# A decoder layer on one core: output projections laid a batch later, W2 steps spread over nine batches, stores on two queues

## The chip, the cores and the metric

The kernel runs on one core of a Trainium2 chip, in float32 throughout. The metric is the device time of one execution in microseconds (us). A core has five engines that run side by side: PE (TensorE, matrix products), DVE (VectorE), ACT (ScalarE), POOL (GpSimd) and SP (SyncE, used here to start DMAs). PE writes to PSUM, a memory of eight banks; the other data lie in SBUF.

## The reference, cut to what matters

One pre-norm decoder layer over x of 16 batches by 112 tokens by 512 features, with 16 heads of 32. A self attention whose heads pass through a small matrix Wdown (32 by 32) and back through Wup, a cross attention over 375 context tokens a batch, and a gated feed-forward part with a Hadamard transform (fwht) between its two halves:

```
x = x + attn(_layernorm(x), Wq, Wk, Wv, Wo, Wdown, Wup)
x = x + xattn(_layernorm(x), ctx_2048, mask, ...)
x = x + ffn(_layernorm(x), W1, W2, W3)

# attn:   q_r, k_r, v_r = heads(x @ W.T) @ Wdown
#         y = softmax(q_r k_r / sqrt(32)) v_r @ Wup;  out = y @ Wo.T
# ffn:    hidden = silu(x @ W1.T) * (x @ W3.T)
#         out = fwht(hidden) @ W2.T
```

## The kernel before, in words

The 1,792 tokens are 14 tiles of 128. Four batches are a group (448 tokens). The residual x stays in `xr`, token by token; `xyT` holds the transposed features that the matrix products read.

*Folding.* Wdown and Wup are made into block-diagonal matrices `bd` (lines 698 to 711), transposed and multiplied (`block_products`, 822), and folded into the query, key and value weights (`fold`, 830). These are the first matrix products of the kernel, mixed with the transposes of the first normalised tiles. The normalised tiles come from `Norm.start` (792): statistics of each tile on DVE (L750, L751), a chain of twelve small DVE operations for the reciprocal root (`rstd_of`, 753), then one operation a tile (L776) into a `row` buffer, `xn`.

*The order of the work.* PE's order is that of the program text: `manual_schedule` is set for PE alone (1495). The instructions of the other engines are put in order by the framework's scheduler, by their place in the program and by when it expects their inputs and buffers. On each engine the order is then fixed. `Filler` (559) spreads other matrix work between the steps of an attention batch: `lay(b, us, *pieces, prepared=n)` (1522) queues pieces and runs batch `b`; `us` says how much of the queue goes between its steps.

*A batch of self attention* (`self_attention`, 986): scores on PE (L908); on DVE two reductions (L996) and two subtractions (L998); on ACT two exponentials (L1001); then, behind the second subtraction on DVE, the store of the batch before (a reciprocal L949 and a product L950) and `prepared` steps of W2. On PE: a first portion of filler, transposes of the exponentials (L1015), filler, transposes, filler, then the products with the values (L919) and the sums (L930).

*Fillers of the self attention.* Queries, keys and values of the next group (`features` L849, `token_rows` L881), transposes of the next normalised tiles (L810), W2's products with a Hadamard matrix (`w2_products`, L1433), and the output projection of finished tiles (`after_self`, 977). A projection needs a PSUM bank of tag `mm`, of which there are two; the bank comes free when DVE has added the result to `xr` (L981). After its last tile `after_self` starts the next norm.

*W2.* `w2_steps` (1444) is a generator of 36 steps. The first 24 each take a `row` buffer for a difference (L1463), make a sum in place (L1464), and let ACT copy the difference back (L1465). The last 12 combine the four parts of W2 (L1477 to L1488) and store blocks to DRAM. All 36 are spread by `prepared`; whatever is left is run out in the loop `for _ in w2_prep`. Once W2 is out, its buffers take the weights of the cross attention (`xk`, `xv`, `xq`, `xo`).

*Row buffers.* `row` (655) gives out four buffers of 128 by 512 under one tag. `xn` of every norm, `diff`, `a`, `e`, `g`, `beta`, `rep`, `d` and the output rows `o` share them.

*The end.* The feed-forward part runs in two passes over the tokens. `output_tile` (1619) transposes a tile of the result back, adds `xr` on DVE (L1625) and stores it by a DMA from SP (L1626), 14 times in all.

Of the kernel before, what the change touches and what calls it, by code (L numbers as in the profile page):

```python
# [14 lines left out]
AF = mybir.ActivationFunctionType  # L15
# [3 lines left out]
P = 128  # L19
# [11 lines left out]
GB = 4  # L31
# [553 lines left out]
def mixed(a, b, skip=0):  # L585

    a, b = iter(a), iter(b)
    for _ in range(skip):
        yield next(a)
    while True:  # L590
        took = [next(p, None) for p in (a, b)]
        if took[0] is None and took[1] is None:
            return
        yield sum(t for t in took if t is not None)
# [3 lines left out]
def finite_layer(  # L598
# [30 lines left out]
    nc = tc.nc  # L629
# [10 lines left out]
    def psum(tag, shape, bufs=2):  # L640
        return ps[""].tile(shape, F32, tag=tag, bufs=bufs, name=tag)

    def weight(name):
        return wt.tile([P, C, D], F32, tag="w", name=name)
# [10 lines left out]
    def row(name):  # L655
        return ln.tile([P, D], F32, tag="row", name=name, bufs=4)
# [5 lines left out]
    def load_weight(w, src):  # L662
        nc.sync.dma_start(out=w, in_=src.rearrange("(c p) n -> p c n", p=P))
# [14 lines left out]
    whole = [range((g * GT) // P, ((g + 1) * GT) // P) for g in range(NG)]  # L678
# [13 lines left out]
    ident = keep.tile([P, P], F32, name="ident")  # L692
# [4 lines left out]

    bd = [keep.tile([P, P], F32, name=f"bd{k}") for k in range(2)]
    bdm = [keep.tile([P, P], F32, name=f"bdm{k}") for k in range(2)]
    diag = ln.tile([P, (4 * TT * 2 + (B + B // 2) * C)], F32, tag="good", name="diag", bufs=1)  # L700
    diag = diag[:, :P].rearrange("p (i d) -> p i d", i=HG)
    nc.gpsimd.memset(diag, 0.0)
    for i in range(HG):
        nc.gpsimd.memset(diag[ts(i, DH), i, :], 1.0)
    for k in range(2):
        nc.vector.tensor_tensor(
            bd[k].rearrange("p (i d) -> p i d", i=HG),
            diag,
            small[:, k, :].unsqueeze(1).to_broadcast([P, HG, DH]),
            ALU.mult,  # L710
        )
# [36 lines left out]
    def stats(src, l, t):  # L748
        st = ln.tile([P, 6], F32, tag="st", name="st")
        nc.vector.bn_stats(st, src)  # L750
        nc.vector.bn_aggr(mv[:, l, t, :], st)  # L751
# [70 lines left out]
    def block_products(k):  # L822
        tr = psum("mm", [P, C, P])
        nc.tensor.transpose(tr[:, 0, :], bd[k], ident)
        nc.scalar.copy(bd[k], tr[:, 0, :])
        nc.tensor.matmul(tr[:, 1, :], bd[0], bd[k], start=True, stop=True)
        nc.scalar.copy(bdm[k], tr[:, 1, :])
        yield 0.5

    def fold(dst, src, block):  # L830

        for m in range(C):
            acc = psum("mm", [P, D])
            for j in range(C):
                if block is None:
                    nc.tensor.transpose(acc[:, ts(j, P)], src[:, j, ts(m, P)], ident)
                else:
                    nc.tensor.matmul(
                        acc[:, ts(j, P)], src[:, j, ts(m, P)], block, start=True, stop=True
                    )  # L840
            nc.scalar.copy(dst[:, m, :], acc)
            yield 0.9
# [46 lines left out]
    def project(w, t, into):  # L889
        acc = psum("mm", [P, D])  # L890
        for c in range(C):
            nc.tensor.matmul(  # L892
                acc, xyT[:, c, ts(t, P)], w[:, c, :], start=(c == 0), stop=(c == C - 1)
            )
            if c == 1:
                yield 1.75
        into(acc)
        yield 1.75
# [78 lines left out]
    def after_self(tiles, norm):  # L977

        for t in tiles:
            yield from project(  # L980
                wo, t, lambda acc: nc.vector.tensor_tensor(xr[:, t, :], acc, xr[:, t, :], ALU.add)  # L981
            )
            stats(xr[:, t, :], norm.l, t)
        norm.start(False)
# [73 lines left out]
    def output_bias():  # L1058


        rep = row("rep")
        repv = rep.rearrange("p (c m) -> p c m", c=C)
        for c in range(C):
            nc.gpsimd.tensor_scalar(repv[:, c, :], ones, bv[:, c : c + 1], None, op0=ALU.mult)
        yield 0.0
        acc = psum("mm", [P, D])
        for c in range(C):
            nc.tensor.matmul(
                acc, repv[:, c, :], xo[:, c, :], start=(c == 0), stop=(c == C - 1)
            )  # L1070
        nc.vector.tensor_tensor(rows["bo"], acc, rows["bo"], ALU.add)
        yield 3.5
# [328 lines left out]
    w2 = []  # L1401
# [15 lines left out]
    def w2_matrix():  # L1417
        h_a = ident
        n, k = 1, 0
        while n < P:  # L1420
            h_b = bd[k]
            a = h_a.rearrange("p (m two n) -> p m two n", two=2, n=n)
            o = h_b.rearrange("p (m two n) -> p m two n", two=2, n=n)
            nc.vector.tensor_tensor(o[:, :, 0, :], a[:, :, 0, :], a[:, :, 1, :], ALU.add)
            nc.vector.tensor_tensor(o[:, :, 1, :], a[:, :, 0, :], a[:, :, 1, :], ALU.subtract)
            h_a = h_b
            n, k = 2 * n, 1 - k
        return h_a

    def w2_products(h, w):  # L1430
        for c in range(0, UNITS, 2):
            acc = psum("mm", [P, D])
            nc.tensor.matmul(  # L1433
                acc, h, w[:, ds(c, 2)].rearrange("p c n -> p (c n)"), start=True, stop=True
            )
            nc.scalar.activation(
                w[:, ds(c, 2)].rearrange("p c n -> p (c n)"),
                acc,
                AF.Copy,
                scale=1.0 / math.sqrt(FF),  # L1440
            )
            yield 0.9
# [55 lines left out]
    n1 = [Norm(0, r) for r in read]  # L1498
    n2 = [Norm(1, r) for r in whole]
    n3 = [Norm(3, r) for r in whole]  # L1500
    grp = [Group(g) for g in range(NG)]
# [3 lines left out]
    for k in range(32):  # L1505
        nc.tensor.transpose(warm[:, 0, ts(k % HG, P)], ident, ident)

    n1[0].start(True)
    f.add(block_products(0), mixed(fold(wq, raws[0], bdm[0]), n1[0].transposes()))
    f.add(grp[0].queries(), fold(wk, raws[1], None))  # L1510
    f.drain()
# [5 lines left out]
    h = w2_matrix()  # L1517
    w2_prep = w2_steps()

    kv = []  # L1520

    def lay(b, us, *pieces, prepared=0):
        f.add(*pieces)
        self_attention(b, grp[b // GB], f, us, prepared)

    lay(0, 15.5, mixed(grp[1].queries(), w2_products(h, w2[0])))
    lay(1, 15.5, mixed(grp[1].keys(), w2_products(h, w2[1])), prepared=6)
    lay(2, 14, mixed(grp[1].values(range(3)), w2_products(h, w2[2])), prepared=6)
    n1[2].start(True)
    lay(  # L1530
        3,
        9.5,
        mixed(grp[1].values(range(3, GB)), w2_products(h, w2[3])),
        n1[2].transposes(),
        prepared=6,
    )

    lay(4, 10.5, after_self(whole[0], n2[0]), prepared=6)
    lay(5, 12, grp[2].queries(), prepared=3)
    lay(6, 13.5, mixed(grp[2].keys(), n2[0].transposes(), 4), prepared=3)  # L1540
    n1[3].start(True)
    lay(7, 15.5, mixed(grp[2].values(range(GB)), n1[3].transposes(), 4), prepared=3)

    lay(8, 14, after_self(whole[1], n2[1]), prepared=3)
    for _ in w2_prep:
        pass
    lay(9, 12, grp[3].queries())
    xk, xv, xq, xo = (weight(n) for n in ("xk", "xv", "xq", "xo"))
    load_weight(xk, c_wk_t)
    load_weight(xv, c_wv_t)  # L1550
    load_weight(xq, c_wq_t)
    load_weight(xo, c_wo_t)
    lay(10, 14, mixed(grp[3].keys(), n2[1].transposes(), 4))
    lay(11, 14, grp[3].values(range(GB)))

    kv.append(Keys(0))
    lay(12, 14, output_bias(), after_self(whole[2], n2[2]))
    lay(13, 11.5, mixed(kv[0].keys(), n2[2].transposes(), 4))
    lay(14, 10.5, kv[0].values())
    kv.append(Keys(1))  # L1560
    qs = [Queries(n) for n in range(B // 2)]
    lay(15, 6, qs[0].pieces())
    pending.store()
# [4 lines left out]
    prepared = []  # L1568
# [50 lines left out]
    def output_tile(p, k):  # L1619
        t = p.n * (2 * GT // P) + k  # L1620
        tr = psum("mm", [P, C, P])
        for c in range(C):
            nc.tensor.transpose(tr[:, c, :], p.out[c // 2][:, c % 2, ts(k, P)], ident)
        o = row("o")
        nc.vector.tensor_tensor(o, tr.rearrange("p c n -> p (c n)"), xr[:, t, :], ALU.add)  # L1625
        nc.sync.dma_start(out=out[ts(t, P), :], in_=o)  # L1626

    def run(*pieces):
        for p in pieces:
# [49 lines left out]
    for u in range(UNITS):  # L1679
        for i in range(2):  # L1680
            p.products(u, i)
            if 2 * u + i < per:
                output_tile(before, 2 * u + i)
# [6 lines left out]
    for k in range(GT // P, per):  # L1690
        output_tile(p, k)


@with_exitstack
def decoder_layer(ctx: ExitStack, tc: tile.TileContext, *args):
    nc = tc.nc
    flag = ctx.enter_context(tc.tile_pool(name="flag", bufs=1))
    unfit = flag.tile([1, 1], I32, name="unfit")
    finite_layer(tc, unfit, *args)
    with tc.If(nc.values_load(unfit, min_val=0, max_val=1, skip_runtime_bounds_check_because="a comparison gives 0 or 1") > 0):  # L1700
        general_layer(tc, *args)
# [49 lines left out]
```

## Time and profile before

| what | value |
|---|---|
| median of three runs | 1429.58 us (1428.09 to 1430.37) |
| profiled execution | 1425.9 us, its span 1423.7 us |
| granted TensorE clock, mean | 0.995 |
| PE busy, 0 to 22 us | 14.40 us |
| PE busy, 22 to 69.4 us | 45.96 of 47.4 us |
| PE busy, 69.4 to 346.9 us (self attention) | 264.4 of 277.5 us |
| PE busy, 346.9 to 1424 us | 1061.8 of 1077.1 us |

The profile is one execution of the program. Its lines name the engine, the source line (L12 is line 12 of the kernel) and the tiles written and read. PE counts two instructions for one float32 product and one for a transpose. "x16" after a line of the timeline means that sixteen instructions in a row are merged. What stands in brackets is the idle time before the first of them and the instruction that ended it. PE's granted clock is below 1 only in the first 22 us and in two later stretches, 143 to 164 us and 311 to 332 us.

### The profile page before, as it was taken

The numbers are of one execution on the slowest core, as the hardware profiler recorded it, in microseconds if no ns is written. First come the engines' busy times: TensorE is split into PE (matmuls) and PEld (weight loads), VectorE is DVE, ScalarE is ACT, GpSimd is POOL, SyncE is SP. The second block draws the span as 40 slices with busy tenths as digits, with TensorE's granted clock in tenths as the row PEclk, the third lists the DMA queues.
The fourth block names the chain that finished last, engine by engine and source line by source line (L and its number), as shares of the span: only waits on it lengthen the run. The fifth ranks groups of instructions, "written<-read, shape, count | busy, mean of one in ns | idle before, by whom it ended". The sixth has DMA issues, their size and how long they took to land.

```text
span 1423.7 us, 19012 instructions
## 1 busy us (share of the span) xinstructions
PE 1386.6 (97%) x8096; PEld 766.7 (54%) x8096; DVE 790.1 (55%) x1340; ACT 365.3 (26%) x560; POOL 30.0 (2%) x46
## 2 busy tenths in 40 slices
PE   7999898999999999999999999999999999999997
PEld 5554454546565656565556565454555555555554
DVE  4058977455665677667665557644734324434332
ACT  2255432324233323332333333111120001111000
POOL 2000010210001000000000000000000000000000
PEclk9999999999999999999999999999999999999999
DMA  8100026101104414321120011222113223521301
GB/s 297 59 1 30 1 75 229 60 23 44 37 30 145 153 37 166 129 97 52 52 82 22 23 35 56 89 89 89 59 63 115 88 96 111 186 102 59 119 1 53
DMA packets 49728, 115.89 MB, mean 81 GB/s; under 512 B 2896, under 2 KB 31584, under 8 KB 41188
## 3 DMA queue, kind: packets, MB, share of 16 engines
q1 hardware_dynamic: 48832, 112.96, 22.2%
q0 software_dynamic: 672, 1.62, 0.4%
q8 instruction: 65, 1.06, 0.3%
q14 instruction: 27, 0.22, 0.0%
q10 hardware_dynamic: 132, 0.02, 0.0%
HBM read 86.80 MB, written 27.79 MB: 80 GB/s over the span
## 4 chain that ended last, share of the span: by engine, by line
PE 90%; DVE 7%; ACT 1%; issue 1%; DMA 0%; DVEq 0%; ACTq 0%
PE mm L849 21%; PE mm L881 14%; PE gate L1349 12%; PE ys L1349 6%; PE mm L892 6%; PE gate L1285 6%; PE mm L1349 5%; PE sc L908 4%; PE ys L919 3%; PE ys L1285 3%; PE mm L1285 3%; PE sc L1015 2%; PE ys L930 2%; PE mm L810 1%; PE mm L1433 1%
## 5 line engine op out<-in xcount | busy, mean ns | idle before, releaser
L881 PE MATMUL mm<-xv,cT 128*125 128x512 f32 x384 | 173.3, 598 | 1.8 <-ACT v L886 1.8
L849 PE MATMUL mm<-cT,xk 128*128 128x375 f32 x512 | 168.8, 485 | 1.3 <-ACT kT L857 1.3
L849 PEld LDWEIGHTS mm<-cT,xk 128*128 128x128 f32 x512 | 95.5, 190 | 71.2 <-issue 11.6
L881 PEld LDWEIGHTS mm<-xv,cT 128*125 128x125 f32 x384 | 70.0, 187 | 81.3 <-issue 73.9
L1349 PE MATMUL gate<-t,f 128*128 128x448 f32 x256 | 101.4, 539 | 0.0
L1139 DVE TENSOR_SCALAR e<-sc,hi 125x896 f32<-125x896 f32 x64 | 70.8, 1144 | 48.6 <-PE sc L908 48.6
L949 DVE RECIPROCAL r<-ys 128x448 f32<-128x448 f32 x32 | 94.3, 2947 | 1.9 <-PE ys L930 1.9
L1142 ACT ACTIVATE e<-e 125x896 f32<-125x896 f32 x64 | 60.9, 951 | 115.5 <-DVE e L1139 82.7
L996 DVE TENSOR_REDUCE mx<-sc 112x8 f32<-112x896 f32 x32 | 33.4, 1084 | 96.7 <-PE sc L908 96.7
L1285 PE MATMUL gate<-h,f 128*128 128x448 f32 x224 | 86.6, 539 | 0.0
L1349 PE MATMUL gate<-xyT,f 128*128 128x448 f32 x192 | 80.1, 540 | 0.0
L1349 PE MATMUL ys<-t,f 128*128 128x448 f32 x192 | 77.4, 539 | 0.0
L1349 PEld LDWEIGHTS gate<-t,f 128*128 128x128 f32 x256 | 48.6, 190 | 47.6 <-issue 47.2
L865 DVE CUSTOM_DVE_ANT_0 junk<-kT 128x375 f32<-128x375 f32 x64 | 34.1, 533 | 64.2 <-ACT kT L857 64.2
L1162 DVE TENSOR_TENSOR es<-es,e 125x896 f32<-125x896 f32 x64 | 68.6, 1089 | 0.4
L1139 DVE TENSOR_SCALAR es<-sc,hi 125x896 f32<-125x896 f32 x32 | 36.6, 1147 | 52.6 <-PE sc L908 45.9
L1285 PEld LDWEIGHTS gate<-h,f 128*128 128x128 f32 x224 | 42.5, 190 | 41.3 <-issue 40.9
L886 ACT COPY v<-mm 125x512 f32<-125x512 f32 (+1 forms) x64 | 37.1, 580 | 104.9 <-PE mm L881 104.8
L908 PEld LDWEIGHTS sc<-q,kT 32*125 32x125 f32 x1536 | 46.2, 183 | 31.9 <-issue 20.5
L857 ACT ACTIVATE kT<-mm,bk 128x375 f32<-128x375 f32 x64 | 36.5, 572 | 91.9 <-PE mm L849 91.9
L892 PE MATMUL mm<-wo,xyT 128*128 128x512 f32 x112 | 52.1, 613 | 7.3 <-DVE xr L981 7.3
L881 PE MATMUL mm<-wv,xyT 128*112 128x512 f32 x128 | 58.0, 596 | 0.3 <-ACT v L886 0.3
(178 smaller groups left out, 1900.2 us busy)
## 6 DMA issues: line engine op xcount, KB each, us to landing
f<-blocks SPq DMA_DIRECT2D x46, 1024.0 KB, 4.8
blocks<-o SPq DMA_DIRECT2D x16, 1024.0 KB, 5.3
cT<-in_ctx SPq DMA_DIRECT2D x16, 750.0 KB, 4.9
o<-in_f_w SPq DMA_DIRECT2D x32, 256.0 KB, 3.2
w<-in_f_w SPq DMA_DIRECT2D x4, 1024.0 KB, 8.7
blocks<-w SPq DMA_DIRECT2D x4, 1024.0 KB, 4.7
out_y<-o SPq DMA_DIRECT2D x14, 256.0 KB, 4.7
xr<-in_x SPq DMA_DIRECT2D x2, 1024.0 KB, 10.2
```

The lines of the kernel that those rows point to most:

```text
L849: nc.tensor.matmul(acc[:, :n], w[:, c, ts(j, P)], src[:, c, :], start=(c == 0), stop=(c == C - 1))
L881: nc.tensor.matmul(acc[:n, :], src[:, c, :], w[:, c, :], start=(c == 0), stop=(c == C - 1))
L886: nc.scalar.copy(dst[:n].rearrange("p h r -> p (h r)"), acc[:n, :])
L892: nc.tensor.matmul(acc, xyT[:, c, ts(t, P)], w[:, c, :], start=(c == 0), stop=(c == C - 1))
L908: nc.tensor.matmul(views[i // 2][:, i % 2, j, :], k_of(i, j), q_of(i, j), start=True, stop=True)
L919: nc.tensor.matmul(y[ts(i, DH), j, :], v[:, HG * j + i, :], es[i // 2][:n, i % 2, j, :], start=first and j == 0, stop=last, skip_group_che ...
L949: nc.vector.reciprocal(r, sums)
L1139: self.clip = nc.vector.tensor_scalar(e[:KP], sc, -CLIP, hi[:, n : n + 1], op0=ALU.max, op1=ALU.min).ins
L1142: nc.scalar.activation(e[:KP], e[:KP], AF.Exp, scale=SCALE)
L1162: nc.vector.tensor_tensor(total, total, late[3][i][:KP], ALU.add)
L1285: nc.tensor.matmul(banks[m][bank], o[:, c, ts(m, P)], t[:, c, :], start=first and c == 0, stop=c == UNITS - 1, skip_group_check=True,)
L1349: nc.tensor.matmul(bank, o[:, s, k, :], t[:, k, :], start=first and k == 0, stop=k == 1, skip_group_check=True,)
```

## The change

It has seven parts.

1. An Exp on one column of `ident` goes to ACT ahead of everything else.
2. The statistics of the first norm are put behind the two products that make `bd` (`made`) on DVE.
3. The W2 steps: six in each of batches 1 to 4 and three in each of 5 to 8 become four in each of batches 1 to 9. The loop that runs out what is left, and with it the last stores of W2, moves behind batch 9.
4. `n1[2].start`, the norm of tiles 7 to 10, moves from behind batch 2 to before it. Its transposes stay in batch 3.
5. The output projections of tiles 0 to 2 move from batch 4 to 5, of tiles 3 to 6 from batch 8 to 9, of tiles 7 to 9 from batch 12 to 13. What they change places with: queries of group 2 (now batch 4), queries of group 3 (now batch 8), and the first cross keys with the output bias (now batch 12). The transposes of the norm after tiles 7 to 9 go into batch 14, with the first cross values.
6. The loads of the first two context blocks (`Keys(0)`, `Keys(1)`) are traced one batch earlier. The transposes of tiles 11 to 13 in batch 7 start after three pieces in place of four.
7. Output tiles of odd `k` are stored by a DMA from ACT in place of SP.

```
@@ -697,13 +697,15 @@
+    nc.scalar.activation(bdm[0][:, :1], ident[:, :1], AF.Exp)
     diag = ln.tile([P, (4 * TT * 2 + (B + B // 2) * C)], F32, tag="good", name="diag", bufs=1)
...
     for k in range(2):
-        nc.vector.tensor_tensor(
+        made = nc.vector.tensor_tensor(
             bd[k].rearrange("p (i d) -> p i d", i=HG),
@@ -1505,7 +1507,8 @@
-    n1[0].start(True)
+    with tc.issue_after(made.ins):
+        n1[0].start(True)
@@ -1524,40 +1527,40 @@
     lay(0, 15.5, mixed(grp[1].queries(), w2_products(h, w2[0])))
-    lay(1, 15.5, mixed(grp[1].keys(), w2_products(h, w2[1])), prepared=6)
-    lay(2, 14, mixed(grp[1].values(range(3)), w2_products(h, w2[2])), prepared=6)
+    lay(1, 15.5, mixed(grp[1].keys(), w2_products(h, w2[1])), prepared=4)
     n1[2].start(True)
+    lay(2, 14, mixed(grp[1].values(range(3)), w2_products(h, w2[2])), prepared=4)
     lay(
         3,
         9.5,
         mixed(grp[1].values(range(3, GB)), w2_products(h, w2[3])),
         n1[2].transposes(),
-        prepared=6,
+        prepared=4,
     )
-    lay(4, 10.5, after_self(whole[0], n2[0]), prepared=6)
-    lay(5, 12, grp[2].queries(), prepared=3)
-    lay(6, 13.5, mixed(grp[2].keys(), n2[0].transposes(), 4), prepared=3)
+    lay(4, 12, grp[2].queries(), prepared=4)
+    lay(5, 10.5, after_self(whole[0], n2[0]), prepared=4)
+    lay(6, 13.5, mixed(grp[2].keys(), n2[0].transposes(), 4), prepared=4)
     n1[3].start(True)
-    lay(7, 15.5, mixed(grp[2].values(range(GB)), n1[3].transposes(), 4), prepared=3)
-
-    lay(8, 14, after_self(whole[1], n2[1]), prepared=3)
+    lay(7, 15.5, mixed(grp[2].values(range(GB)), n1[3].transposes(), 3), prepared=4)
+
+    lay(8, 12, grp[3].queries(), prepared=4)
+    lay(9, 14, after_self(whole[1], n2[1]), prepared=4)
     for _ in w2_prep:
         pass
-    lay(9, 12, grp[3].queries())
...
     lay(10, 14, mixed(grp[3].keys(), n2[1].transposes(), 4))
+    kv.append(Keys(0))
     lay(11, 14, grp[3].values(range(GB)))
-    kv.append(Keys(0))
-    lay(12, 14, output_bias(), after_self(whole[2], n2[2]))
-    lay(13, 11.5, mixed(kv[0].keys(), n2[2].transposes(), 4))
-    lay(14, 10.5, kv[0].values())
+    lay(12, 12.5, mixed(kv[0].keys(), output_bias(), 4))
+    lay(13, 14, after_self(whole[2], n2[2]))
     kv.append(Keys(1))
+    lay(14, 12.5, mixed(kv[0].values(), n2[2].transposes(), 2))
@@ -1623,7 +1626,7 @@
-        nc.sync.dma_start(out=out[ts(t, P), :], in_=o)
+        (nc.scalar if k % 2 else nc.sync).dma_start(out=out[ts(t, P), :], in_=o)
```

## The prediction

> **What bounds the kernel now.** I read the page first, then the list of who waited for whom on PE, then a table by stage, then the order of PE and DVE inside the stages that lose time.
>
> The page: PE is busy 97% of the span.
>
> ```profile
> span 1423.7 us, 19012 instructions
> PE 1386.6 (97%) x8096; PEld 766.7 (54%) x8096; DVE 790.1 (55%) x1340; ACT 365.3 (26%) x560; POOL 30.0 (2%) x46
> ```
>
> So 37 us at most are idle on PE, and the change adds and removes no matmul: only holes can pay. PE's waits inside the self attention (60 to 345 us):
>
> ```profile
> PE mm L892 <- DVE xr L981: 7.3, 2, 4.0
> PE mm L810 <- ACT kT L857: 2.9, 1, 2.9
> PE sc L1015 <- ACT e L1001: 1.2, 1, 1.2
> PE mm L810 <- ACT xyT L811: 1.1, 1, 1.1
> ```
>
> The table by stage shows where they lie: batch 4 (from 143.20), batch 8 (217.30), batch 9 (239.00) and batch 13 (311.20); the columns after the name are busy time and count, then the granted PE clock. Two of the holes also pull the clock down.
>
> ```profile
> 143.20:163.70 20.50, 16.53 (x116) 8.32 (x112) 19.94 (x29) 8.43 (x12) 0.00 (x0) 0.92 0.00 1
> 217.30:239.00 21.70, 18.41 (x128) 9.31 (x124) 16.81 (x24) 3.71 (x4) 0.00 (x0) 1.00 0.55 204
> 239.00:256.80 17.80, 16.61 (x124) 9.14 (x120) 11.43 (x23) 5.63 (x8) 0.00 (x0) 1.00 0.56 214
> 311.20:331.80 20.60, 17.69 (x136) 11.46 (x132) 13.87 (x30) 7.65 (x11) 4.11 (x3) 0.92 0.00 0
> ```
>
> PE's timeline in batch 4 (start, length, what, idle before it): third tile of the output projection waits 3.97 us for a PSUM bank, and then runs at half clock, 3.59 us where 1.90 is usual.
>
> ```profile
> 151.13 0.93 PE L1015 MATMUL sc<-ident,e 112*112 112x112 f32 x8
> 156.03 3.59 PE L892 MATMUL mm<-wo,xyT 128*128 128x512 f32 x4 [3.97 <-DVE xr L981]
> 159.46 0.93 PE L1015 MATMUL sc<-ident,e 112*112 112x112 f32 x8
> 160.23 1.90 PE L892 MATMUL mm<-wo,xyT 128*128 128x512 f32 x4
> ```
>
> And DVE just before and in it. The reader is to see two things: six W2 steps (L1463, L1464) run only after PE's transposes released their rows at 138, although their batch began at 128; and the add that frees the bank (L981, 155.29) stands behind them.
>
> ```profile
> 125.36 0.54 DVE L776 TENSOR_SCALAR xn<-xr,seen,rstd 128x512 f32<-128x512 f32 x1
> 126.42 1.45 DVE L776 TENSOR_SCALAR xn<-xr,seen,rstd 128x512 f32<-128x512 f32 x3
> 138.20 0.69 DVE L1463 TENSOR_TENSOR diff<-w 128x512 f32<-128x512 f32 x1 [1.23 <-PE mm L810]
> 146.16 2.08 DVE L996 TENSOR_REDUCE mx<-sc 112x8 f32<-112x896 f32 x2
> 150.15 2.95 DVE L949 RECIPROCAL r<-ys 128x448 f32<-128x448 f32 x1
> 155.29 0.68 DVE L981 TENSOR_TENSOR xr<-mm,xr 128x512 f32<-128x512 f32 x1
> ```
>
> **The sum before.** Batch 2: 0.3. Batch 3: 0.3 + 1.1. Batch 4: 4.0, and 1.7 of slow clock (3.59 less 1.90). Batch 8: 3.3. Batch 9: 1.2. Batch 13: 2.9, and about 1.7 of slow clock (one group of four L849 took 2.53 where its neighbours take 1.43; two groups of transposes 0.7 more together). Sum 16.5 us. The opening loses more: queries start at 21.33.
>
> **What the Trainium skill says.** "TensorE: Matmul & The Clock Gate", Part 1: the clock falls to half after an idle window of some 3.4 us that runs freely, so the same hole may or may not cost it. The trace agrees in kind: a 2.91 us hole (batch 13) cost clock and a 3.29 us hole (batch 8) did not. "DMA: Bandwidth & Descriptors", Issuing engines are not separate DMA queues: DMAs of several engines run on the same 16 engines, and a second issuer only saves issue time. The issue here is 0.332 us for each store. "ScalarE: Activation LUTs", What ACT_TABLE_LOAD costs: a load belongs to a change of set. The trace has one load at 1.92 us (1.28 us long) and one at 886.96, none at the first Exp at 73.58.
>
> **Part by part.** *Exp at the head and the stores.* The Exp moves no load that is left, and ACT is idle until 11.11: nothing. The last four stores are issued 0.65 us apart from SP, which needs 0.332 each; the last is k=6, which stays on SP, and takes 4.7 us to land. Nothing; between -0.5 and +0.5 us. In the second pass ACT may wait for an odd row, but its copies have about 3 us of slack (three products of 1.08 before the bank is needed again): nothing.
>
> *Wdown blocks first.* Now PE waits 2.78 us for bd (L706, at 10.40, behind the statistics). Behind the landing of a_up (issue 1.28 + 6.7 = 7.98) bd could be there at 8.3. But the statistics then start at 8.35 in place of 6.37; their own work (2.95 + 2.15 + 0.48) puts the first xn at 13.9, where the first transpose is now too (13.94). Gain: the first fold is over by then, so the second starts at 14.45 in place of 14.82, and the chain of fold, copy and transpose behind it (1.84 us a round) brings the queries to 20.6: 0.7 us won. Bounds -0.3 (if a_up lands a microsecond later) and +1.0.
>
> *n1[2] a batch earlier, W2 steps at four.* Rows of tag "row" (four) are handed out in program order: xn of n1[2] was ready at 31 us, but came at 125, behind batch 2's sixth diff. Its new place is before batch 2. So it takes all four rows after batch 1 and keeps them till its transposes at the end of batch 3 (137.6). Batch 2's four steps and batch 3's four wait for that: eight from 138.2 in place of six. At the measured 8.0/6 = 1.33 us a step they end at 148.8, and batch 4's first reduction waits behind them, 4.7 us after its scores (144.15). In batch 9 a delay of 3.37 us (243.32 less 239.95) cost 1.20, since four pieces of queries (6.28 us) lie in front; batch 4 has just these now. So it loses 4.7 - 2.2 = 2.5, and 0.5 for a chance of slow clock. Bounds: 0 if the reductions are let in between the steps, 9 if the steps go one row at a time.
>
> *Projections of tiles 0 to 2 in batch 5.* DVE has no backlog there (batch 4: 4.1 softmax + 3.5 store + 4 x 1.22 = 12.5 us in a batch of over 16). L981 comes 9.8 us after the first reduction, as measured (146.16 to 155.97): two thirds of it are reductions, subtractions and the reciprocal. PE asks for the bank 7.9 us after the scores. 2.0 lost, 0.3 for clock. In batch 6 the keys put 7.6 us in front, enough for the norm's chain.
>
> *Tiles 3 to 6 in batch 9.* Before, in batch 8, five W2 operations stood ahead of L981 and cost 3.3. Now the last four steps hold eight; the last one waits for a row, so seven go ahead: 3.3 + 2 x 0.6 = 4.4, and 1.1 for clock. Bounds 0 and 6. Batch 10's keys hide the delay that cost batch 9 its 1.2.
>
> *Tiles 7 to 9 in batch 13, cross keys in 12.* No norm runs ahead of batch 12, so the 2.9 and 1.7 go. In 13 no W2 step is left: L981 ends 7.7 to 8.3 us after the reductions start, PE asks at 7.9: 0.3. In 14 the chain of rstd and xn (5.6 us behind the last tile, 3.4 of it under transposes, values and scores) delays the reductions by 2.2; three pieces (5.7 us) stand in front of exponentials that need 2.2 + 4.1: 0.6.
>
> *Loads.* xk to xo come after batch 9 or earlier, by 258 us at the latest, and land in about 12: 30 us before batch 12. cT of batch 0 still waits for batch 11's scores. SP has under 1 us of issues in any batch there. Nothing.
>
> **The sum after.** 0.3 + 1.4 + 3.0 + 2.3 + 5.5 + 0.3 + 0.6 = 13.4. Won 16.5 - 13.4 = 3.1 in the self attention and 0.7 at the head: 3.8. The profiled execution took 1425.9 (span 1423.7 and 2.2 around it) and would take 1422.1; the median of the runs is 3.7 higher, so 1425.8.
>
> **The rivals.** *B, the bank comes free in time.* If L981 is put directly behind the store (7.7 us), batches 5 and 9 lose nothing, and batch 4 loses 1.0 with the reductions let in: 0.3 + 1.4 + 1.0 + 0.3 + 0.6 = 3.6, won 12.9 + 0.7, 1416.0. For it: in batch 4 L981 was let in after three operations. Against: batch 8, after five.
> *C, given back.* The clock falls in all three holes (1.7 each: 3.2 more than taken) and the head wins nothing: 1429.7. For it: two of four holes cost clock before.
> *D, slower.* The eight held steps get their rows one by one: diff, add and ACT's copy (0.62) in a line, some 2.2 us with the waits. The reduction of batch 4 then starts at 155.8, 11.6 after its scores; 9.4 lost and 1.7 of clock in place of 3.0: 1433.9. It decides from about 2.0 us a step. Against: the six of batch 3 took 1.33.
> That the blocks are not earlier, since a_up's DMA is what they wait for, is inside the bound of the head.
>
> **How the numbers follow.** Main case 0.48 (own range 1423 to 1428), B 0.20, C 0.20, D 0.12. Faster by over 0.2% (2.9 us, about what a measurement of this kernel can tell from no change): 0.41 of the main case and B, 0.61. Within: 0.07 and 0.18, 0.25. Slower: D and the rest of C, 0.14. The range 1416 to 1431 leaves out D and about a third of B.
>
> **What would show it.** Held diffs (L1463) with no W2 step in batch 2; the first reduction of batch 4 some 4 us behind its scores; PE's waits for L981 of 2 us in batch 5 and 4 in batch 9; none in batch 12; bd before the first statistics and the queries at 20.6. If W2 steps do run in batch 2, rows are not handed out in order, and batch 4's loss is not there. If L981 stands elsewhere, B or C holds.

## The result and the profile after

The changed kernel takes 1433.07 us (median; 1431.62 to 1434.67), the kernel before on the same chip 1428.43 (1423.96 to 1431.22). The ratio is 1.0034, 95% interval 1.0023 to 1.0046: slower by a third of a per cent. The profiled execution has a span of 1430.7 us, 7.0 more than before, with nearly the same mean granted clock (0.994, before 0.995). The medians differ by 4.6 only, since the profiled execution of the kernel before (1425.9) was one of its faster ones; what follows explains the 7.0 between the two profiles. From here on the line numbers are those of the changed kernel unless the kernel before is named. They are two higher than before at the places that matter: the projection's product is L894 (was L892), its add L983 (L981), the copy of the self attention's keys L857 (L855; the L857 of the kernel before, in the prediction's list, is the copy of the cross keys).

The page after: the work is the same, PE has 2.8 us more busy time, and the rest of the 7 us is idle.

```profile
span 1430.7 us, 19016 instructions
PE 1389.4 (97%) x8096; PEld 767.2 (54%) x8096; DVE 789.2 (55%) x1340; ACT 365.4 (26%) x561; POOL 30.4 (2%) x46
```

PE's waits inside the self attention, after (60 to 345 us; who waits, for whom, then total, number and longest in us):

```profile
PE mm L894 <- DVE xr L983: 9.6, 2, 5.1
PE mm L812 <- ACT kT L857: 1.8, 2, 1.1
PE mm L812 <- ACT v L888: 1.2, 1, 1.2
PE mm L812 <- ACT xyT L813: 1.2, 1, 1.2
PE mm L851 <- ACT kT L857: 0.8, 1, 0.8
PE ys L921 <- ACT eT L1019: 0.7, 1, 0.7
PE sc L1017 <- ACT e L1003: 0.5, 1, 0.5
```

Two more lines of 0.3 each, for `v`, stand in the views of both kernels. Before, the first line was 7.3. The wait for the projection's add did not go: it moved with the projection and grew. Four lines with `kT`, `v` and `eT`, 4.5 us together, are waits for ACT's copies.

The batches show where the 7 us came from. The durations in this table are worked out from the starts of the scores (L908, now L910) in PE's timeline, in us; "start" is the first score of batch 0. The three columns at the right belong to experiments below.

| | before | after | e2 | e10 | e5 |
|---|---|---|---|---|---|
| start | 69.4 | 70.3 | 69.8 | 69.3 | 67.1 |
| batch 4 | 20.5 | 17.1 | 17.1 | 16.5 | 16.4 |
| batch 5 | 16.4 | 21.1 | 14.7 | 20.4 | 14.7 |
| batch 6 | 17.8 | 20.0 | 24.6 | 19.7 | 18.7 |
| batch 8 | 21.7 | 16.4 | 16.4 | 16.4 | 16.4 |
| batch 9 | 17.8 | 25.6 | 18.1 | 18.1 | 18.1 |
| batch 10 | 18.2 | 19.5 | 20.0 | 19.5 | 18.3 |
| batch 13 | 20.6 | 15.9 | 15.9 | 15.9 | 15.9 |
| batch 14 | 14.7 | 17.9 | 17.9 | 17.9 | 17.1 |

The batches left out (0 to 3, 7, 11, 12) differ by 0.1 us at most among these five. Summed from unrounded starts: head +0.9; batches 4 and 5, which changed places, +1.3; 6 +2.3; 8 and 9 +2.5; 10 +1.3; 12 to 14 -1.5; the end +0.2. That is the 7.0.

PE's timeline of the changed kernel in batch 5 and the hole of batch 9 (start, length, what; in brackets the idle time before it):

```profile
162.22 7.13 PE L894 MATMUL mm<-wo,xyT 128*128 128x512 f32 x16
169.20 0.93 PE L1017 MATMUL sc<-ident,e 112*112 112x112 f32 x8
174.62 3.64 PE L894 MATMUL mm<-wo,xyT 128*128 128x512 f32 x4 [4.49 <-DVE xr L983]
...
252.19 5.82 PE L894 MATMUL mm<-wo,xyT 128*128 128x512 f32 x8 [5.09 <-DVE xr L983]
```

It is the picture of batch 4 before. In batch 5 two tiles run, the third waits, and then the clock is at half: 3.64 for four instructions where 1.90 is usual, 5.82 for eight where 3.70 is. What DVE did in that time in batch 5:

```profile
162.33 2.09 DVE L998 TENSOR_REDUCE mx<-sc 112x8 f32<-112x896 f32 x2 [0.33 <-PE sc L910]
...
166.33 2.95 DVE L951 RECIPROCAL r<-ys 128x448 f32<-128x448 f32 x1
169.19 0.63 DVE L1465 TENSOR_TENSOR diff<-w 128x512 f32<-128x512 f32 x1
169.74 0.61 DVE L952 SCALAR_TENSOR_TENSOR xyT<-ys,r 128x448 f32<-128x448 f32 x1
170.27 0.68 DVE L1466 TENSOR_TENSOR w<-w 128x512 f32<-128x512 f32 x1
170.86 1.29 DVE L1465 TENSOR_TENSOR diff<-w 128x512 f32<-128x512 f32 x2
172.07 1.29 DVE L1466 TENSOR_TENSOR w<-w 128x512 f32<-128x512 f32 x2
173.27 0.69 DVE L1465 TENSOR_TENSOR diff<-w 128x512 f32<-128x512 f32 x1
173.87 0.69 DVE L983 TENSOR_TENSOR xr<-mm,xr 128x512 f32<-128x512 f32 x1
```

Seven operations of W2 (count the x after L1465 and L1466: 1, 1, 2, 2, 1) stand ahead of the add that PE waits for. In batch 9 there are eight, between 246.16 and 251.44. The first product had ended at about 166, so the add could have run at 169.2, behind the reciprocal. DVE was never idle here; its order was wrong for PE.

### The profile page after: what moved, and what is told of

Read it like the earlier page. It is cut to its first block, busy times and chain, and to the rows that moved or that the text cites. A ratio compares the mean times of both kernels' runs of the same rounds, so it can differ in the third digit from the quotient of the medians.

```text
span 1430.7 us, 19016 instructions
## 1 busy us (share of the span) xinstructions
PE 1389.4 (97%) x8096; PEld 767.2 (54%) x8096; DVE 789.2 (55%) x1340; ACT 365.4 (26%) x561; POOL 30.4 (2%) x46
## 4 chain that ended last, share of the span: by engine, by line
PE 88%; DVE 8%; ACT 2%; issue 1%; DMA 0%; ACTq 0%; DVEq 0%; POOLq 0%
PE mm L851 20%; PE mm L883 13%; PE gate L1351 12%; PE ys L1351 6%; PE mm L894 6%; PE gate L1287 6%; PE mm L1351 5%; PE sc L910 4%; PE ys L921 3%; PE ys L1287 3%; PE mm L1287 3%; PE ys L932 1%; PE sc L1017 1%; DVE st L752 1%; PE mm L1435 1%
## 5 line engine op out<-in xcount | busy, mean ns | idle before, releaser
L894 PE MATMUL mm<-wo,xyT 128*128 128x512 f32 x112 | 54.2, 635 | 9.6 <-DVE xr L983 9.6
L910 PEld LDWEIGHTS sc<-q,kT 32*125 32x125 f32 x1536 | 46.2, 183 | 31.9 <-issue 19.8
## 6 DMA issues: line engine op xcount, KB each, us to landing
xr<-in_x SPq DMA_DIRECT2D x2, 1024.0 KB, 10.5
```

What stands on the lines that cost most here:

```text
L894: nc.tensor.matmul(acc, xyT[:, c, ts(t, P)], w[:, c, :], start=(c == 0), stop=(c == C - 1))
L910: nc.tensor.matmul(views[i // 2][:, i % 2, j, :], k_of(i, j), q_of(i, j), start=True, stop=True)
```

## The experiments

A ratio is against the kernel before on the same chip. Where only a span is given, there is one run, and its parts are compared inside the trace.

**e1: the statistics first again.** The changed kernel, without the wait for `made`:

```
-    with tc.issue_after(made.ins):
-        n1[0].start(True)
+    n1[0].start(True)
```

> The changed kernel with the first statistics no longer put behind the Wdown and Wup blocks. Theory (the statistics, 2 us late, cost more than the earlier blocks bring): the first xn is there at 12.5 us in place of 14.5, PE's wait of 3.3 us for it goes, and the scores of batch 0 start at 69.4 in place of 70.3; span 1429.8. Rival (the head is neutral, the 0.9 us come from somewhere else): batch 0 still starts at 70.3.

Measured: span 1431.3. Batch 0 begins at 69.07, 1.2 us earlier, so the order at the head does cost (the last section compares all the heads). But batches 5 and 9 took 22.2 and 26.2 for 21.1 and 25.6, with the very same waits (4.49 and 5.09). In batch 5 the granted clock was 0.85 in place of 0.92. In batch 9 it was 0.87 in both, but more of the slow stretch fell on products (6.40 us for the eight behind the hole, 5.82 before this edit). The gain at the head is shown, and the total doesn't show it.

**e3: the norm of tiles 7 to 10 behind batch 2 again.** Only `n1[2].start(True)` moves back behind `lay(2, ...)`. It asks whether the held rows, which push W2 steps together, are what puts them ahead of the add.

> The changed kernel with the norm of tiles 7 to 10 started behind batch 2 again, as before. Theory (its four rows hold up the W2 steps of batches 2 and 3, which then run into batches 4 and 5): W2 steps run in batch 2 again, batch 4 loses its wait of 0.5 us, and the add of batch 5 comes after four W2 operations in place of seven, so its wait is 2.5 to 3 us in place of 4.5; span about 1428. Rival (the held rows cost nothing): batch 5 waits 4.5 us again; span 1430.5.

Measured: span 1431.2. Batch 4 takes 16.4 and loses nothing, so its 0.7 did come from the held rows. The wait of batch 5 did not move; PE's timeline of this kernel:

```profile
173.49 3.78 PE L894 MATMUL mm<-wo,xyT 128*128 128x512 f32 x4 [4.49 <-DVE xr L983]
```

Seven operations still stand ahead. My explanation for batch 5 fell: the steps' own place ahead of the projection decides, not their backlog.

**e2: the W2 steps behind the filler.** In `self_attention`, the steps are traced after the first portion of filler, so that the scheduler sees the projection's adds first:

```
             pending.store()
-            for _ in range(prepared):
-                next(w2_prep, None)
         first = max(0.45 * us, min(us, 5.5))
         f.fill(first)
+        with tc.issue_after(behind.ins):
+            for _ in range(prepared):
+                next(w2_prep, None)
```

> The changed kernel with the W2 steps of a batch traced behind the first portion of filler, so that on DVE they stand behind the adds that free the projection's PSUM banks. Theory (W2 operations ahead of the add are what PE waits for): PE's waits for the add in batches 5 and 9 (4.5 and 5.1 us) fall under 0.6 each, their slow clock (1.7 and 2.1) goes, batch 5 takes 15.5 us in place of 21.1 and batch 9 about 19 in place of 25.6; span about 1418.5. Rival (reductions, subtractions and the reciprocal alone make the add late): 2.5 us or more of wait is left in each; span about 1425.

Measured: 1424.09 against 1427.32, ratio 0.9977 (0.997 to 0.9984), now faster than before. DVE of this kernel in batch 5:

```profile
161.82 2.09 DVE L998 TENSOR_REDUCE mx<-sc 112x8 f32<-112x896 f32 x2 [0.34 <-PE sc L910]
...
165.82 2.95 DVE L951 RECIPROCAL r<-ys 128x448 f32<-128x448 f32 x1
168.69 0.63 DVE L983 TENSOR_TENSOR xr<-mm,xr 128x512 f32<-128x512 f32 x1
```

The add is done 7.5 us after the first reduction began (161.82 to 169.32), where the changed kernel took 12.2 (162.33 to 174.56). Batch 5 takes 14.7 and batch 9 18.1 (the table): both waits are gone. But 4.6 of it came back in batch 6, most of it as one wait:

```profile
189.30 1.08 PE L812 MATMUL mm<-ident,xn 128*128 128x128 f32 x4 [4.46 <-DVE xn L778]
```

The steps now run among the statistics of the norm that follows the projection, and `xn` comes at 188.61. A stall was removed and the next thing in DVE's queue became late.

**e4: no W2 steps in the projection batches.** Six each in batches 1, 2, 6 and 8, none in 5 and 9, with the loop that runs out the rest before batch 9. If the steps themselves are to blame, both batches must be as short as in e2.

> The changed kernel with the W2 steps of batches 5 and 9 given to batches 1, 2, 6 and 8 (six in each), so that the batches with projections have none. Theory (W2 operations ahead of the add): as in the run with the steps behind the filler, waits under 0.6 us in batches 5 and 9; ten held steps now end in batch 4, which waits 1 to 3 us for its exponentials; span about 1420. Rival (softmax and store alone make the add late): 2.5 us or more left in each; span about 1427.

Measured: span 1426.8. Batches 5 and 9 take 14.7 and 18.1, as in e2. But six steps in batch 2 wait for the rows that `n1[2]` holds, and more of them fall on batch 4, which takes 23.2 with a wait of 3.6 for its exponentials (expected 1 to 3) and a granted clock of 0.85, and batch 7 takes 23.4 with a wait of 2.1 for `v`. The cause in 5 and 9 is shown twice now; where the steps are put in their place matters as much.

**e7: the norm behind the projection later.** In the changed kernel, `after_self` no longer starts the norm. The next batch starts it under the same `issue_after` as the store, behind its own subtractions, and the transposes of batches 6, 10 and 14 come two pieces of filler later (the norm in the cross attention keeps its place):

```
+        late_norms.append(norm)
+
+    def started(norm):
+        late_norms.remove(norm)
         norm.start(False)
+        yield 0.0
...
         with tc.issue_after(behind.ins):
+            while late_norms:
+                late_norms.pop().start(False)
             pending.store()
...
-    lay(6, 13.5, mixed(grp[2].keys(), n2[0].transposes(), 4), prepared=4)
+    lay(6, 13.5, mixed(grp[2].keys(), n2[0].transposes(), 6), prepared=4)
```

> The changed kernel with the norms after a projection started behind the next batch's subtractions, and their transposes two pieces later; W2 steps as in the changed kernel. Theory (the norm's chain delays the exponentials, and ACT's copies that free PE's banks stand behind these): the waits of batches 6 (0.8 and 0.7), 10 (1.1) and 14 (1.2) for kT and v go, batch 6 takes about 18 us in place of 20.0 and batch 10 about 18.2 in place of 19.5; the waits for the add in 5 and 9 stay at 4.5 and 5.1; span about 1426. Rival (the banks are late for another reason): 1 us or more is still lost in each of the three; span about 1430.

Measured: span 1428.4. Batches 6, 10 and 14 take 18.7, 18.3 and 17.1 for 20.0, 19.5 and 17.9; the waits for `kT` and `v` are gone, a wait of 0.8 for `xn` is left. So the norm's chain did delay the exponentials. The edit moves the transposes too, but ACT shows that the exponentials and copies came earlier: in batch 6 the copy behind the second exponential ended 7.8 us after the first score (190.14 less 182.31), and 10.5 us after it in the changed kernel (192.81 less 182.34). How the norm delays them is seen in the changed kernel's batch 6. On DVE the chain's last operation stands between the two subtractions:

```profile
187.89 1.09 DVE L1000 TENSOR_TENSOR e<-sc,mx 112x896 f32<-112x896 f32 x1
188.89 1.45 DVE L778 TENSOR_SCALAR xn<-xr,seen,rstd 128x512 f32<-128x512 f32 x3
190.26 1.08 DVE L1000 TENSOR_TENSOR e<-sc,mx 112x896 f32<-112x896 f32 x1
```

On ACT the copy that frees the keys' bank stands behind the exponential of the second:

```profile
191.44 0.95 ACT L1003 ACTIVATE e<-e 112x896 f32<-112x896 f32 x1 [1.06 <-DVE e L1000]
192.29 0.52 ACT L857 COPY kT<-mm 128x448 f32<-128x448 f32 x1
```

And PE waits for the copy:

```profile
192.86 0.66 PE L812 MATMUL mm<-ident,xn 128*128 128x128 f32 x4 [0.66 <-ACT kT L857]
```

**e8: one block ahead of the statistics, all stores from SP.** PE's first need is Wdown's block alone, and `a_up` lands after `a_down`:

```
-    for k in range(2):
-        made = nc.vector.tensor_tensor(
+    def make_block(k):
+        return nc.vector.tensor_tensor(
...
+    made = make_block(0)
...
         n1[0].start(True)
+    make_block(1)
```

> The changed kernel with only the Wdown block ahead of the first statistics, the Wup block behind them, and all stores on SP again. Theory (it is Wup's block, whose load lands at 8.4 us, that holds up the statistics): the first xn is there at 12.8 us in place of 14.5, the scores of batch 0 start at 68.5 in place of 70.3. The stores: from DVE's last operation to the end of the span 6.8 us as with two queues, plus or minus 0.3. Rival (the landing of Wdown's block holds them up too, or two queues do shorten the end): batch 0 at 69.5 or later; the end over 7.3 us.

Measured: span 1429.9. Batch 0 begins at 68.69, 1.6 us earlier. The changed kernel's DVE at the head:

```profile
8.44 0.29 DVE L708 TENSOR_TENSOR bd<-diag,small 128x128 f32<-128x128 f32 x1 [1.61 <-DMA small<-in_a_up]
8.65 1.28 DVE L752 BATCH_NORM_STATS2 st<-xr 128x6 f32<-128x512 f32 x2
...
13.96 1.92 DVE L778 TENSOR_SCALAR xn<-xr,seen,rstd 128x512 f32<-128x512 f32 x4
```

and PE's:

```profile
10.18 1.13 PE L840 MATMUL mm<-bdm,raw_q 128*128 128x128 f32 x8 [0.48 <-DMA raw_q<-in_a_wq]
14.56 1.11 PE L812 MATMUL mm<-ident,xn 128*128 128x128 f32 x4 [3.26 <-DVE xn L778]
15.47 1.91 PE L840 MATMUL mm<-bdm,raw_q 128*128 128x128 f32 x8
```

The second block waits 1.61 us for `a_up`, and everything behind it with it. With one block ahead the first `xn` begins at 12.44, and PE's wait is 1.95.

**e6: the kernel before, with its W2 steps behind the filler.** The edit of e2 alone. It asks whether the order of the batches was needed at all.

> The kernel before, with the W2 steps traced behind the first portion of filler, nothing else. Theory (W2 operations ahead of the add, in the old order as in the new): the waits for the add in batches 4 and 8 (4.0 and 3.3 us) fall under 0.6, the slow clock of batch 4 (1.7) goes, batch 13 keeps its 2.9; span about 1415. Rival (the steps pushed back delay the softmax of batches 5 and 9): half of it is given back there; span about 1420.

Measured: 1419.97 against 1427.71, ratio 0.9944 (0.9928 to 0.9961). Batch 8 takes 18.1 for 21.7. Batch 4 gains only 1.7 us, for another wait stood behind the first:

```profile
154.31 3.10 PE L892 MATMUL mm<-wo,xyT 128*128 128x512 f32 x4 [2.17 <-DVE xyT L950]
```

Tile 2 of the projection contains tokens of batch 3, whose store is made in batch 4 itself. A projection in batch 4 thus depends on that store, and one a batch later doesn't. PE asks 8.9 us after the batch's first score (152.14 less 143.25), and the store ended 11.0 after it. But the store was that late because four W2 operations, held from batch 3, ran from 143.79 to 146.24, ahead of the first reduction. In batch 5 of e2, where the first reduction follows the scores directly, the store ends 9.1 us after the first score. So most of this wait is W2's as well, and what the order is worth once W2 is out of the way of the reductions too was not measured. Batches 4 and 5 together take 37.0 before, 36.7 here, 38.2 after the change, 31.8 in e2. The wait of 2.9 in batch 13, which the changed order removes, is still there (20.6 us, 15.9 after the change).

**e10 and e11: the two halves of the change apart.** e10 is the kernel before with the changed order of batches (parts 5 and 6 of the change, and the Exp of part 1, with 6 and 3 W2 steps, the statistics first, the norm in its old place and all stores from SP). e11 is the kernel before with four W2 steps in each of batches 1 to 9 alone.

```
-    lay(4, 10.5, after_self(whole[0], n2[0]), prepared=6)
-    lay(5, 12, grp[2].queries(), prepared=3)
+    lay(4, 12, grp[2].queries(), prepared=6)
+    lay(5, 10.5, after_self(whole[0], n2[0]), prepared=3)
...
-    lay(8, 14, after_self(whole[1], n2[1]), prepared=3)
+    lay(8, 12, grp[3].queries(), prepared=3)
...
+    lay(9, 14, after_self(whole[1], n2[1]))
```

> The changed kernel with only its order of batches left: head, W2 steps (six in batches 1 to 4, three in 5 to 8), norm of tiles 7 to 10 and stores as before. Theory (the order pays, and W2 steps in the batches with projections spoil it): batch 9, now with no step, takes 18.1 us in place of 25.6; batch 5 waits about 3.3 us behind five W2 operations and takes about 18.5; batches 6 and 10 keep their 20.0 and 19.5; span about 1419. Rival (the order itself is what loses): batches 4 to 14 together take as long as in the changed kernel, 209 us from the scores of batch 4 to those of 15; span about 1429.

> The kernel before with only the W2 steps spread as in the change, four in each of batches 1 to 9. Theory (what counts is how many operations stand ahead of the add): batch 4, with a smaller backlog and two operations ahead of the add in place of three, waits about 1.5 us in place of 4.0 and takes about 17 in place of 20.5; batch 8, with six ahead in place of five, waits about 4 in place of 3.3; span about 1420. Rival (spreading the steps is what loses in the change): batches 4 to 9 take longer than before (113.6 us from the scores of batch 4 to those of 10); span over 1424.

Measured for e10: 1422.27 against 1428.37, ratio 0.9957 (0.9943 to 0.9971). The order alone pays. It pays in batches 8 and 9, together 34.6 us for 39.5, because the projection of batch 9 now has no W2 step beside it, and in batches 12 to 14 (1.5). Batches 4 and 5 take 36.9 as before, and 6 and 10 lose 3.2. Batch 5, with three W2 steps, keeps a wait:

```profile
PE mm L894 <- DVE xr L983: 3.8, 1, 3.8
```

Five W2 operations stand ahead of it there. Against e10 (span 1420.3) the changed kernel has 10.4 us more, and 7.5 of them are batch 9.

Measured for e11: span 1422.8. Batches 4 to 9 take 115.8 us, before 113.6, so the spread alone costs there: batch 8 takes 24.0 for 21.7, with a wait of 3.9. But the head was 1.3 us shorter, with no edit of it, and batch 13 took 1.7 less with the same wait of 2.9. Both are the clock: it was granted at 1.00 in the first 30 us and in batch 13, where the kernel before had 0.94 and 0.92. So the total says nothing either way.

**e5 and e9: all of it together.** e5 is the changed kernel with e2, e7, e3 and e8's head, and with W2 steps moved from batches 5 and 9 (two each) to 1 and 8 (six each). e9 is e5 with all stores from SP.

```
-    lay(5, 10.5, after_self(whole[0], n2[0]), prepared=4)
+    lay(5, 10.5, after_self(whole[0], n2[0]), prepared=2)
...
-    lay(9, 14, after_self(whole[1], n2[1]), prepared=4)
+    lay(9, 14, after_self(whole[1], n2[1]), prepared=2)
```

> The changed kernel with everything that the runs so far point to: W2 steps behind the first filler, two of them in place of four in batches 5 and 9 (six in 1 and 8), the norms after a projection started behind the next batch's subtractions with their transposes two pieces later, the norm of tiles 7 to 10 back behind batch 2, and only the Wdown block ahead of the first statistics. Theory (DVE's order makes PE's waits): no wait over 1.5 us in batches 4 to 15, batch 5 about 15 us, 6 about 18, 9 and 10 about 18.3 each; scores of batch 0 at 68.5, of batch 15 at 334 in place of 353.4; span about 1411. Rival (the work is only pushed from wait to wait): batches 6, 10 and 14 take over 2 us more each; span about 1419.

> The run with everything that the runs point to, and all stores on SP again. Theory (two queues make the end longer: 6.8 to 7.2 us from DVE's last operation in seven profiles with two, 6.4 to 6.6 in three with SP alone): 6.5 us, span about 1409.4, 0.4 less than with two queues. Rival (that difference is chance): 6.9 us or more.

Measured: e5 1411.45 against 1427.71, ratio 0.9886 (0.9869 to 0.9902); e9 1412.07 against 1428.37, ratio 0.9881 (0.9864 to 0.9897). Both beat the kernel before and the change. PE's waits of e5 inside the self attention, all that are left:

```profile
PE mm L814 <- ACT xyT L815: 1.5, 2, 1.1
PE ys L923 <- ACT eT L1031: 1.4, 3, 0.7
PE mm L814 <- DVE xn L780: 0.8, 1, 0.8
PE mm L885 <- ACT v L890: 0.3, 1, 0.3
PE mm L1447 <- ACT v L890: 0.3, 1, 0.3
```

The head gives 3.2 us of the 20.9 that lie between the spans of the change and of e5 (1409.8), batch 9 7.5, batch 5 6.4, batches 4, 6, 10 and 14 together 4.0: 21.1. About 1.1 of the head is the clock and not the edit: e9, with the same head, begins batch 0 at 68.17 with a granted clock of 0.94 in the first 30 us, e5 at 67.06 with 1.00.

## Why the prediction was wrong

Forecast were 1425.8 us and a gain of 3.8; measured was a loss of 7.0 in the span (4.6 in the medians). The sum by its own steps:

| step | forecast | measured |
|---|---|---|
| head | -0.7 | +0.9 |
| batches 4 and 5 | -0.4 | +1.3 |
| batch 6 | 0 | +2.3 |
| batches 8 and 9 | +1.0 | +2.5 |
| batch 10 | 0 | +1.3 |
| batches 12 to 14 | -3.7 | -1.5 |
| end | 0 | +0.2 |

The 10.8 us between -3.8 and +7.0 are no single step's: batches 6 and 10, which the prediction put at nothing, make 3.6 of them, batches 4, 5, 8 and 9 3.2, batches 12 to 14 2.2, the head 1.6 and the end 0.2.

*What held.* The rows are handed out in order: no W2 step ran in batch 2, and the first held `diff` came at 139.08. Batch 12 lost nothing. PE did wait for the add in 5 and 9, and loads cost nothing.

*Batches 5 and 9, mis-sized.* The step that failed is "L981 comes 9.8 us after the first reduction, as measured". It came after 12.2, with seven W2 operations behind the reciprocal and not three. I had measured the distance in a batch whose softmax itself had started late: in batch 4 of the kernel before, four of the seven W2 operations between the scores and the add ran ahead of the first reduction, which the prediction shows at 146.16:

```profile
143.71 1.33 DVE L1463 TENSOR_TENSOR diff<-w 128x512 f32<-128x512 f32 x2
144.95 1.29 DVE L1464 TENSOR_TENSOR w<-w 128x512 f32<-128x512 f32 x2
...
153.02 0.63 DVE L1463 TENSOR_TENSOR diff<-w 128x512 f32<-128x512 f32 x1
...
154.09 0.68 DVE L1464 TENSOR_TENSOR w<-w 128x512 f32<-128x512 f32 x1
154.69 0.68 DVE L1463 TENSOR_TENSOR diff<-w 128x512 f32<-128x512 f32 x1
```

From the first score to the end of the add it was 12.8 us there and 13.3 in batch 5; the distance from the reduction was the wrong one to carry over. Against the 14.7 us of e2 and e4, batch 5 lost 6.4 where I had 2.3. In batch 9 the wait was 5.09 for my 4.4 and the clock took 2.1 for my 1.1; against the 18.1 of e2, e4 and e10 it lost 7.5 for my 5.5. Eight W2 operations went ahead of the add there and not seven: my own sum, 3.3 + 0.6 for each one more than five, gives 5.1 for eight (and 4.5, not 4.4, for seven). The reason "DVE has no backlog there" also answered the wrong question: an add can be late on an engine without a backlog, if the order puts other work in front of it. e2, e4 and e10 show the W2 steps as the cause; e3 rules out the held rows.

*Batch 4, too much.* Forecast were 3.0 lost; the wait was 0.48, and e3 gives 0.7 in all. The reductions were let in between the steps, as the lower bound had it. This hid 2.3 of the 4.1 that batch 5 lost more.

*Batches 6 and 10, wrong mechanism.* "In batch 6 the keys put 7.6 us in front, enough for the norm's chain" and "Batch 10's keys hide the delay" are the steps that failed most clearly, 3.6 us together against a forecast of nothing. I counted filler as time that PE can spend. But a piece of keys needs a bank that ACT's copy frees, and ACT works in order: the copy stands behind the exponential, the exponential behind the subtraction, the subtraction behind the norm's chain on DVE. e7 moved only the norm and its transposes, and got back 1.4 of the 2.3 us of batch 6 and 1.2 of the 1.3 of batch 10. Where the other 0.9 of batch 6 comes from stays open.

*The head, wrong sign.* The second `bd` was made at 8.44 (forecast 8.3). But 13.96 is where the first `xn` begins, and the 13.9 of the forecast was where it ends: the statistics began at 8.65 for 8.35, and the chain of the reciprocal root took 0.2 more than my sum has. So the first transposes ran at 14.56 and not at 13.94. Nor did "the chain of fold, copy and transpose" run in the time measured before: PE had stood for 3.26 us and ran these transposes in 1.11 and the next fold in 1.91, where the fold ahead of the wait took 1.13 and e8's first transposes 0.66. The queries started at 22.21 and not at 20.6. e1 puts the cost of the order at 1.2 us, e8 that of the second block at 1.6; since the head differs between kernels with the same order too (below), the sizes are rough.

*Batches 12 to 14.* The wait of 2.9 is gone, as forecast. New waits are 0.73 in batch 13 and 1.44 in 14, for my 0.3 and 0.6. PE's busy time in the three batches fell by 0.8 us (50.53 to 49.77), not by the 1.7 that I had put down to the clock. The 1.7 itself was right: e11, which has the old order there and a clock of 1.00, is busy for 48.86. The changed kernel, also at 1.00, needs 0.9 more than that, and why stays open.

*The rivals.* The sign was that of D (1433.9), and so nearly was the time, but that is chance: D's mechanism, rows one at a time in batch 4, did not happen. C was right that the clock falls in the holes and the head wins nothing; the hole in batch 4 that it counted was not there. B asked for the add directly behind the store; that is what e2 makes in batches 5 and 9. It paid 0.23% by itself against B's 1%, since batch 6 gave 4.6 us back until the norm was moved as well (e5).

## What to carry to other kernels

Before work that an engine does in the background is spread evenly, look for the operations on that engine that free a buffer for the critical one, and trace the background behind them: here two lines moved in the kernel before gave 0.56%. When a stall depends on a distance measured in another place, count the operations that will stand in front in the new place, not the time that passed in the old. Filler in front of a wait is only cover if its own buffers come free without the thing that is late.

## What the runs showed of the hardware

The slow clock behind a hole has no fixed price. Batch 5 with the same wait of 4.49 us took 21.1 us in the changed kernel and in e7, and 22.2, 22.1 and 21.8 in e1, e3 and e8. The granted clock parts them: 0.92 over the batch in the first two, 0.84 to 0.85 in the other three. Its shortfall times the length of the batch is 1.7 us in the first two and 3.3 to 3.5 in the others, so the slow stretch was about twice as long. A wait of 2.9 us in batch 13 went with a clock of 0.92 in the kernel before and of 1.00 in e11. The Trainium skill ("TensorE: Matmul & The Clock Gate", Part 1) says that the window runs freely and that the count of slow products varies from run to run; these traces agree, and put the spread at about 1 us in batch 5. The page also has a whole idle window of some 3.4 us come before the slow clock, as the prediction repeats. Here the measurement differs: in e6 a hole of 2.17 us in batch 4 was enough for the next four instructions to take 3.10 us for 1.90.

Most of the spread between executions goes with the clock too. The 22 executions of the kernel before beside e1 to e4 run from 1423.93 us (granted 0.997) to 1430.95 (0.990). The four of e5, with hardly a hole left, run from 1411.14 to 1412.50 (0.997 to 0.999).

The head shows the same. In the first 30 us the granted clock was 0.94 in every kernel but e5 and e11, which had 1.00. At 0.94 batch 0 began at 69.8 to 70.3 in the five kernels with the changed order at the head (the change, e2, e3, e4, e7), at 69.1 to 69.5 in four with the old one (before, e1, e6, e10), and at 68.2 to 68.7 in two with one block ahead (e8, e9). At 1.00 it began at 68.0 with the old order (e11) and at 67.1 with one block ahead (e5). So the changed order costs between 0.3 and 1.2 us, one block ahead gains against the old order, and the clock is worth about as much as either (1.0 to 1.6 us).

Stretches with the clock at full speed repeat far better: batch 8 took 16.4 in every kernel of the table but the one before, which had other work there.

Stores on two queues ended no earlier. From DVE's last operation to the end of the span the kernels with all stores from SP took 6.4 to 6.7 us, those with two queues 6.8 to 7.2. The skill ("DMA: Bandwidth & Descriptors", Issuing engines are not separate DMA queues) has a second issuer save issue time alone; here no saving reached the end of the span, and e5 and e9 differ by less than can be told.
